# Moving half of two input groups into the next phase, merging two dimensions of the block scaling, and shifting a residual, a load and two coefficient chains in a convolution-scan kernel

## The chip, the cores and the metric

The kernel runs on one core of one Trainium2 chip. The metric is the device time of one execution in microseconds (us); the time of a kernel is the median of its runs.

## The reference

The input x has shape 32 x 48 x 64 x 128 (images, channels, rows, columns), fp32. Two layers are applied, each `x = x + conv(gn(x))`, where `gn` normalizes each image over groups of three channels, and `conv` is a chain of four scans. In each scan a line of the image is replaced by itself plus a 5-tap convolution over all 48 channels of the line before it, plus a bias:

```python
def step(w, b):
    def f(carry, inp):
        nxt = inp + _conv1d(carry, w, b)
        return (nxt, nxt)
    return f
...
_, d_rest = jax.lax.scan(step(down_w, down_b), d0, xs[1:])      # 64 rows, downwards
_, u_rest = jax.lax.scan(step(down_w, down_b), u0, seq)         # 64 rows, upwards
_, r_rest = jax.lax.scan(step(right_w, right_b), r0, ws[1:])    # 128 columns, rightwards
_, l_rest = jax.lax.scan(step(left_w, left_b), l0, R[Ww - 2::-1])  # 128 columns, leftwards
...
x = x + _L0_conv_ref(_gn(x), ...)
x = x + _L1_conv_ref(_gn(x), ...)
```

Each line needs the line before it, so the scans are one long chain of steps; only different images are independent.

## The kernel before

The 32 images are cut into four groups of eight (groups 0 to 3; the input of group g is called "input g" here and `x{g}` in the code). Row scans take one group at a time, column scans a pair of groups. `PHASES` (L103) puts them one after the other: phase 0 rows of group 0, phase 1 rows of group 1, phase 2 columns of pair 0, phase 3 rows of group 2, phase 4 rows of group 3, phase 5 columns of pair 1, and phases 6 to 11 the same for layer 1 (10 and 11 are the two column phases). Phases 8 and 9 are `JOINED` (L117): the downward scan of one group runs step by step together with the upward scan of the group before it; these are the joint scans.

A step (`step`, L904) is nine matrix products per scan direction and tile on TensorE (PE, L917) and three additions on VectorE (DVE, L931) that write the new line in place; the next step's products read them. In the program's names `step_02d` is layer 0, group 2, downwards; `00r` is layer 0, pair 0, rightwards; a number behind it is the line, and upward and leftward scans count down.

Everything else is put beside the steps by an agenda: `at(t, fn, ...)` asks for a function at step unit t, where a unit is one step (phase 1 starts at unit 126, phase 2 at 252, phase 3 at 506, phase 4 at 632). The agenda fixes the order of the instructions of each engine, and each engine runs its own in that order. Almost all DMAs are issued by SyncE (SP) from one queue; an issue whose data are not ready, or whose buffer is still in use, holds back all behind it.

What the change touches:

- `plan_input` (L1047) brings the raw input of groups 1 to 3 into the kernel's own layout, in six pieces of 2 MB. For each piece `take_in` (L658) loads it (DMA in_x to the buffer `nat`), `permute` (L675) reorders it in 16 copies on GpSimd (POOL), `put_out` (L677) stores it in four DMAs to the DRAM tensor `xin`, and `stats.take_others` takes sums on ScalarE (ACT, L544 to L536). Groups 2 and 3 have one buffer `nat`, so the next piece is loaded when the one before is used up. After the last piece `scaling` (L390) turns the sums into the scale and offset of the normalization: a chain of small operations over DVE (L561, L576, L465, L483, L495), PE (L401, L412), POOL and ACT. `spread` issues one of its operations per unit; its argument `slack` chooses between a short form on DVE (0) and a longer one that also uses POOL (8).
- `plan_rows` (L1067): `move_rows` (L713) loads 16 rows at a time from `xin` (20 DMAs; `ahead` says how many units before the scan, for each of the four blocks) and `scale_rows` (L753) normalizes them in place on ACT (24 activations at L760). In the joint scans blocks of eight rows are scaled. The result of a row phase is stored eight rows at a time by ten DMAs each (`upa` in layer 0); phase 0's stores are spread over phase 1, from unit 44 of it on.
- The seam between a row phase and a column phase (`send_row`, `send_rest`, L796, and `hold_queue`, L821): the first columns of pair 0 are gathered from the rows just finished by 91 small DMAs from on-chip memory to on-chip memory (`arena<-arena`). Half of them are issued by SP, behind all its stores. The first step rightwards waits for them.
- `plan_cols` (L1125): when a column phase is over, the result gets its residual in 24 units: `load_residual`, `add_residual` on POOL (L852), `keep_result` (a 1 MB store to `mid`), and sums for the next layer's normalization (on DVE for the first group of the pair, on ACT at L613 to L619 for the second). The last six of them (j = 0) come after the phase has ended, beside the next row phase. Then follow the two coefficient chains `r0` and `r1` (r2 and r3 for pair 1) for layer 1.

Of the kernel before, what the change touches and what calls it, by code (L numbers as in the profile page):

```python
# [41 lines left out]
GB = 8  # L42
# [35 lines left out]
def weight_runs():  # L78
# [24 lines left out]
PHASES = (  # L103
    ("rows", 0, 0),
    ("rows", 0, 1),
    ("cols", 0, 0),
    ("rows", 0, 2),
    ("rows", 0, 3),
    ("cols", 0, 1),
    ("rows", 1, 0),  # L110
    ("rows", 1, 1),
# [9 lines left out]
def kernel(  # L121
# [528 lines left out]
    x_masks = [mask_x]  # L650
# [38 lines left out]
    def row_views(k):  # L689
        return [slot[i].rearrange("p (o h n) -> p o h n", o=NG, h=HALF) for i in slots(k)]  # L690

    def place(k, h):


        first = k
        while first in JOINED:
            first -= 1
        since = k - first
        turned = (since + 1) // 2 % 2 if h < HALF else since % 2
        c = h % HALF // E8  # L700
        return HALF // E8 - 1 - c if turned else c

    def rows_at(k, h0, h1):

        places = sorted(place(k, h) for h in range(h0, h1, E8))
        at = places[0] * E8 + h0 % E8
        assert h0 // HALF == (h1 - 1) // HALF and places[-1] - places[0] == len(places) - 1
        return row_views(k)[h0 // HALF][:, :, at : at + h1 - h0]

    def row(k, h):  # L710
        return rows_at(k, h, h + 1)[:, :, 0]
# [41 lines left out]
    def scale_rows(k, h0, h1, groups=range(NG)):  # L753
        _, layer, g = PHASES[k]
        scale, offset = coeffs[layer, g]
        view = rows_at(k, h0, h1).rearrange("p o h (k b) -> p o b h k", b=GB)
        for o in groups:
            for b in range(GB):
                args = view[:, o, b], scale[:, o, b : b + 1], offset[:, o, b : b + 1]
                nc.scalar.activation(  # L760
                    args[0], args[0], AF.Identity, bias=args[2], scale=args[1]
                )
# [271 lines left out]
    def at(t, fn, *args):  # L1034
        agenda.append((t, len(agenda), fn, args))

    def spread(t, gen, every):


        def go(t):  # L1040
            if next(gen, "end") != "end":
                at(t + every, go, t + every)
                agenda.sort(key=lambda a: a[:2])

        at(t, go, t)

    def plan_input(g, times, work, lag, nats, perms):  # L1047

        stats = InputStats(f"x{g}", 0)
        rows = nats[0].shape[-1] // W  # L1050
        ahead, pieces_of = len(nats), rows * W // BN
        per = rows * W * GB // perms[0].shape[-1]
        for j, t in enumerate(times):
            nat = nats[j % ahead]
            if j == 0 and g > 1:
                at(t - 7, take_in, g, 0, nat)
            for i in range(per):
                perm, r = perms[i % len(perms)], i * rows // per
                at(t + i * work / per, permute, nat, r, perm, [nc.gpsimd])
                at(t + i * work / per + 4, put_out, g, rows * j + r, perm)  # L1060
            at(t + lag, stats.take_others, pieces_of * j, nat)
            if j + ahead < len(times):
                free = t + 7
                at(free, take_in, g, rows * (j + ahead), nat)
        spread(t + work + lag + (0, 2, 40, 32)[g], scaling(f"x{g}", 0, g, stats, x_masks, (0, 0, 8, 8)[g]), 1)

    def plan_rows(k, t0, prev):  # L1067
        down, up = (2 if k in JOINED else 1), (2 if k + 1 in JOINED else 1)
        t_up = t0 + down * (H - 1)
        if k == 1:  # L1070
            ahead, scaled = (-34, -18, -3, 12), (-12, -2, 17, 33)
        elif prev == "cols":
            ahead, scaled = (-28, -12, 4, 20), (-13, 3, 19, 35)
        else:
            ahead, scaled = (-54, -43, 0, 11), (-22, -8, 16, 30)
        if k in JOINED:
            for i in range(H // E8):
                h, t = i * E8, t0 + 2 * i * E8
                for o in range(NG):
                    at(t - 34 + 2 * o, take_rows, k, h, h + E8, o)  # L1080
                at(t - 17, scale_rows, k, h, h + E8)
        elif k:
            for i in range(4):
                if PHASES[k][1]:
                    for o in range(NG):
                        t = t0 + ahead[i] - 2 + 3 * o
                        at(t, take_rows, k, i * LOAD, (i + 1) * LOAD, o)
                else:
                    at(t0 + ahead[i], move_rows, k, i * LOAD, (i + 1) * LOAD, False)
                at(t0 + scaled[i], scale_rows, k, i * LOAD, (i + 1) * LOAD)  # L1090

        cuts = list(range(0, H + 1, E8))
        following = PHASES[k + 1][0] == "cols"
        seam = following and follows(k + 1)
        if seam:
            cuts = cuts[2:]
            end = t_up + up * (H - 1)
            at(end - E8, move_rows, k, E8, 2 * E8, True, 0)
            for h in range(E8 - 1, -1, -1):
                at(end - h, send_row, k + 1, h, range(0, E8 // 2))  # L1100
            at(end, send_rest, k + 1, range(E8 // 2, E8))
            for q in range(1, NQ):
                at(end + 0.1 if q == 1 else end + 1.6, move_rows, k, 0, 2 * E8, True, q)
        for h0, h1 in zip(cuts, cuts[1:]):
            t = t_up + up * (H - 1 - h0)
            if k == 0:
                t += 16 if h0 >= HALF else 68
            elif up == 2:
                t += 1
            elif not following:  # L1110
                t = t_up + 29 + 5 * (H - h1) / E8 + (34 if h1 <= HALF else 0)
            at(t, move_rows, k, h0, h1, True)
        at(
            t_up,
            nc.gpsimd.tensor_copy,
            last.rearrange("p (o n) -> p o n", o=NG),
            row(k, H - 1),
        )

    def follows(k):  # L1120

        _, layer, pair = PHASES[k]
        return PHASES[k - 1] == ("rows", layer, 2 * pair + 1)

    def plan_cols(k, t0, prev):  # L1125
        _, layer, pair = PHASES[k]
# [23 lines left out]
        end = left + W - 1  # L1150
        for i in range(n):

            t = left + 64 + 2 * i if layer == 0 else left + 39.5 + 4.5 * i
            at(t, spill_unit, k, i, True)
        units = []
        for n_done, j in enumerate((3, 2, 1, 0)):
            first, every = left + 34 + 32 * n_done, 4.5
            if j == 0 and PHASES[k + 1 if not final else k][0] == "rows":
                first, every = end + 29, 6
            units += [(first + every * i, j, i) for i in range(n)]  # L1160
        stats = None
        if layer == 0:
            stats = ResultStatsV(f"r{2 * pair}"), ResultStatsA(f"r{2 * pair + 1}")
# [6 lines left out]
        for u, (t, j, i) in enumerate(direct):  # L1170
            nat = tiles[u % n]
            o, half = UNITS[i]
# [24 lines left out]
                if u >= 2 and u - 2 + n < len(direct):  # L1197
                    at(t + 4.6, load_residual, k, *direct[u - 2 + n][1:], tiles[(u - 2) % n])
        if layer == 0:
            t = units[-1][0] + 14  # L1200
            g = 2 * pair
            spread(t, scaling(f"r{g}", 1, g, stats[0], r_masks, 8), 1)
            spread(t + 20, scaling(f"r{g + 1}", 1, g + 1, stats[1], r_masks, 8), 1)
# [24 lines left out]
    starts, end = [], 0  # L1228
    for k, (kind, *_) in enumerate(PHASES):
        n = (H if kind == "rows" else W) - 1  # L1230
        starts.append(end - 2 * n if k in JOINED else end)
        end = starts[-1] + (2 if k in JOINED else 1) * n + (2 if k + 1 in JOINED else 1) * n
    for k, (kind, layer, _) in enumerate(PHASES):
        (plan_rows if kind == "rows" else plan_cols)(k, starts[k], PHASES[k - 1][0])

    def wide_nat(i0, n):
        return arena[:, i0 : i0 + GB * n * W].rearrange("p (b m) -> p b m", b=GB)

    tiles = [stage[:, i] for i in range(4)]
    nats1 = [wide_nat(2 * SLOT + i * UNIT * 2, 4) for i in range(4)]  # L1240
    plan_input(1, [starts[0] + 44 + 7.5 * j for j in range(6)], 5, 1, nats1, tiles[2:4])
    nats = [wide_nat(3 * SLOT, 4)]
    times = [starts[1] + 24 + 9.5 * j for j in range(6)]
    plan_input(2, times, 6, 6, nats, tiles[2:4])
    times = [starts[2] + 60 + 13.5 * j for j in range(6)]
    plan_input(3, times, 6, 6, nats, tiles[2:4])

    def more_weights(key, layer, way):
# [12 lines left out]
    def first_group():  # L1261
# [124 lines left out]
        def scale_shared(h0, h1):  # L1386
            scale_rows(0, h0, h1, range(1))
            for o in range(1, NG):
                scale_at_once(0, h0, h1, pool, o, o + 1)
# [124 lines left out]
```

## Time and profile before

| | |
|---|---|
| time, median of 3 runs | 4370.5 us (4369.97 to 4374.02) |
| the profiled execution | 4372.83 us |
| its span, first to last instruction | 4371.1 us |
| mean granted TensorE clock | 0.968 |
| PE busy | 4063.2 us, 93% of the span |
| DVE, ACT, POOL busy | 2071.2, 1303.0, 829.9 us (47%, 30%, 19%) |
| DMA | 680.83 MB, 156 GB/s |

The profile was taken on one execution. A row of a timeline gives the start of a stretch of like instructions, how long the stretch lasted, engine, line and operation, the number of instructions, and in brackets the idle time ahead of it with what ended it. A row of a window gives each engine's busy time in it, then the granted clock, the mean busy share of the 16 DMA engines and GB/s. For SP (`SPq`) a row is the time over which a run of DMAs was issued, not the transfer itself. PE is busy for 93% of the span, so a change shows either as idle time of PE that goes or comes, or not at all.

### The profile page before, as it was taken

What the parts mean: (1) busy time and instruction counts of PE and PEld (TensorE: products, weight loads), DVE (VectorE), ACT (ScalarE), POOL (GpSimd) and SP (SyncE); (2) the same over time, 40 slices, a digit from 0 to 9 for tenths busy, and PEclk for the clock granted to TensorE, in tenths of its full rate; (3) what the DMA queues carried; (4) which work ended last, traced back from release to release, by engine and by line L of the source; (5) the groups of instructions that cost most, each with busy time, mean ns of one, the idle gap of its engine ahead of it and who ended that gap; (6) DMA issues with size and microseconds to landing.
All of it is one profiled execution on the core that took longest, in us unless ns stands there. A gap on an engine that the chain in (4) does not pass through costs nothing. (4 is left out here: it accounts for less than half of the span.)

```text
span 4371.1 us, 86080 instructions
## 1 busy us (share of the span) xinstructions
PE 4063.2 (93%) x34456; PEld 3962.1 (91%) x34456; DVE 2071.2 (47%) x6119; ACT 1303.0 (30%) x2632; POOL 829.9 (19%) x775
## 2 busy tenths in 40 slices
PE   7999929999999999999999997777899999999994
PEld 5999929999999999999999986666799999999994
DVE  6454414447664444446655432222244444444444
ACT  5646310336855100005773423223200002210022
POOL 5722220233220000004220000000000005530253
PEclk9999969999999999999999998988999999999997
DMA  9887797859989455807988845534389416999799
GB/s 291 235 168 166 181 163 144 247 154 263 197 164 151 72 99 108 206 1 217 216 152 137 128 76 80 82 63 79 56 136 176 115 49 165 290 269 164 137 241 192
DMA packets 2213584, 680.83 MB, mean 156 GB/s; under 512 B 2013776, under 2 KB 2162496, under 8 KB 2188608
## 3 DMA queue, kind: packets, MB, share of 16 engines
q1 hardware_dynamic: 2069056, 582.37, 65.0%
q10 hardware_dynamic: 141568, 87.46, 8.3%
q0 software_dynamic: 2560, 5.51, 0.5%
q8 instruction: 271, 4.44, 0.4%
q14 instruction: 129, 1.06, 0.1%
HBM read 398.29 MB, written 295.14 MB: 159 GB/s over the span
## 5 line engine op out<-in xcount | busy, mean ns | idle before, releaser
L760 ACT ACTIVATE arena<-arena,offset,scale 128x256 f32<-128x256 f32 (+2 forms) x936 | 589.8, 723 | 620.2 <-DVE arena L931 187.2
L852 POOL TENSOR_TENSOR arena<-arena 128x2048 f32<-128x2048 f32 x80 | 362.8, 4550 | 1493.8 <-PE step_10l L917 474.1
L917 PE MATMUL step_00r<-arena,early 128*128 128x128 f32 x2286 | 252.3, 274 | 78.4 <-DMA arena<-arena 77.6
L917 PEld LDWEIGHTS step_00r<-arena,early 128*128 128x128 f32 x2286 | 251.2, 185 | 79.1 <-issue 77.9
L675 POOL COPY arena<-arena 128x256 f32<-128x256 f32 x340 | 201.2, 651 | 416.3 <-DMA arena<-in_x 237.1
L613 ACT ACTIVATE early<-arena 128x256 f32<-128x256 f32 x192 | 129.6, 675 | 440.2 <-POOL arena L852 433.9
L917 PE MATMUL step_01r<-arena,early 128*128 128x128 f32 x2286 | 250.7, 273 | 7.0 <-DMA arena<-arena 5.9
L917 PEld LDWEIGHTS step_01r<-arena,early 128*128 128x128 f32 x2286 | 250.0, 185 | 7.7 <-issue 6.0
L917 PE MATMUL step_00l<-arena,wleft 128*128 128x128 f32 x2286 | 249.2, 272 | 0.0
L917 PE MATMUL step_11r<-arena,early 128*128 128x128 f32 x2286 | 249.2, 272 | 0.0
L917 PEld LDWEIGHTS step_11r<-arena,early 128*128 128x128 f32 x2286 | 248.6, 184 | 0.5 <-DVE arena L931 0.3
L917 PEld LDWEIGHTS step_00l<-arena,wleft 128*128 128x128 f32 x2286 | 248.7, 184 | 0.0
L917 PE MATMUL step_11l<-arena,wleft 128*128 128x128 f32 x2286 | 248.5, 272 | 0.0
L917 PE MATMUL step_10l<-arena,wleft 128*128 128x128 f32 x2286 | 248.5, 272 | 0.0
L917 PE MATMUL step_01l<-arena,wleft 128*128 128x128 f32 x2286 | 248.4, 272 | 0.0
L917 PE MATMUL step_10r<-arena,early 128*128 128x128 f32 x2286 | 248.4, 272 | 0.0
L917 PEld LDWEIGHTS step_10l<-arena,wleft 128*128 128x128 f32 x2286 | 248.4, 184 | 0.0
L917 PEld LDWEIGHTS step_11l<-arena,wleft 128*128 128x128 f32 x2286 | 248.4, 184 | 0.0
L917 PEld LDWEIGHTS step_01l<-arena,wleft 128*128 128x128 f32 x2286 | 248.4, 184 | 0.0
L917 PEld LDWEIGHTS step_10r<-arena,early 128*128 128x128 f32 x2286 | 248.4, 184 | 0.0
L931 DVE SCALAR_TENSOR_TENSOR arena<-step_00r,bd,arena 128x128 f32<-128x128 f32 x381 | 122.1, 348 | 209.5 <-PE step_00r L917 126.3
L874 ACT COPY arena<-arena 128x256 f32<-128x256 f32 x172 | 99.6, 656 | 368.8 <-POOL arena L852 243.5
(568 smaller groups left out, 6865.3 us busy)
## 6 DMA issues: line engine op xcount, KB each, us to landing
xin<-arena SPq DMA_DIRECT2D x94, 512.0 KB, 4.1
arena<-in_x SPq DMA_DIRECT2D x18, 2048.0 KB, 9.8
arena<-xin SPq DMA_DIRECT2D x96, 384.0 KB, 9.7
upb<-arena SPq DMA_DIRECT2D x192, 192.0 KB, 3.9
arena<-upb SPq DMA_DIRECT2D x96, 384.0 KB, 11.4
arena<-xin SPq DMA_DIRECT2D x174, 192.0 KB, 4.3
mid<-arena SPq DMA_DIRECT2D x32, 1024.0 KB, 11.6
upa<-arena SPq DMA_DIRECT2D x168, 192.0 KB, 3.9
```

The source lines that it names most:

```text
L613: nc.scalar.activation(junk[:, 0:n], view[:, b], AF.Identity, accum_out=self.sum[:, i, j : j + 1])
L675: copy(dst[:, r, q], src[:, r0 + r, q])
L760: nc.scalar.activation(args[0], args[0], AF.Identity, bias=args[2], scale=args[1])
L852: eng.tensor_tensor(unit, unit, nat, ALU.add)
L874: copy(by_w(perm)[:, a], src[:, a])
L917: nc.tensor.matmul(part(whole(ps[o])[0:m], -s), weights[:, i, at : at + m], part(src(i), s), start=seen[o] == 1, stop=seen[o] == left[o],)
L931: nc.vector.scalar_tensor_tensor(to, sums, bd[:, o, layer, way : way + 1], term, ALU.add, ALU.add)
```

## The change

There are five edits.

1. `scale_rows`: rows and the elements of a row are named as one merged dimension, `(h k)` in place of `h k`.
2. `plan_input`: for groups 2 and 3 every piece's load is placed seven units ahead of its permutation (before: the first only, and the others seven units behind the permutation of the piece before). The coefficient chain starts 2 (group 2) and 5 (group 3) units after the last piece, in place of 40 and 32, and group 3's chain has slack 0 in place of 8.
3. The six pieces of input 2 were all in phase 1, 9.5 units apart; now three are in phase 1, 16 apart from unit 28, and three in phase 2, 13 apart from unit 60. The six of input 3 were all in phase 2; now three are in phase 2 from unit 106 and three in phase 3 from unit 42.
4. `plan_rows`: where a row phase of layer 0 follows a row phase (phase 4; phase 1 has its own numbers), the first two blocks of rows are loaded 46 and 32 units ahead in place of 54 and 43.
5. `plan_cols` of pair 0: the six last residual units start at unit 3 behind the phase's end, 7 apart (before: 29 and 6), and the chains r0 and r1 start 70 units behind the last residual unit in place of 14.

```diff
@@ scale_rows
-        view = rows_at(k, h0, h1).rearrange("p o h (k b) -> p o b h k", b=GB)
+        view = rows_at(k, h0, h1).rearrange("p o h (k b) -> p o b (h k)", b=GB)
@@ plan_input
-            if j == 0 and g > 1:
-                at(t - 7, take_in, g, 0, nat)
+            if g > 1:
+                at(t - 7, take_in, g, rows * j, nat)
...
-            if j + ahead < len(times):
-                free = t + 7
-                at(free, take_in, g, rows * (j + ahead), nat)
-        spread(t + work + lag + (0, 2, 40, 32)[g], scaling(f"x{g}", 0, g, stats, x_masks, (0, 0, 8, 8)[g]), 1)
+            if g == 1 and j + ahead < len(times):
+                at(t + 7, take_in, g, rows * (j + ahead), nat)
+        t += work + lag + (0, 2, 2, 5)[g]
+        spread(t, scaling(f"x{g}", 0, g, stats, x_masks, (0, 0, 8, 0)[g]), 1)
@@ plan_rows
             ahead, scaled = (-54, -43, 0, 11), (-22, -8, 16, 30)
+            if not PHASES[k][1]:
+                ahead = (-46, -32, 0, 11)
@@ plan_cols
-                first, every = end + 29, 6
+                first, every = (end + 29, 6) if pair else (first, 7)
...
-            t = units[-1][0] + 14
+            t = units[-1][0] + (14 if pair else 70)
@@ the times of the pieces
-    times = [starts[1] + 24 + 9.5 * j for j in range(6)]
+    times = [starts[1] + 28 + 16 * j for j in range(3)]
+    times += [starts[2] + 60 + 13 * j for j in range(3)]
     plan_input(2, times, 6, 6, nats, tiles[2:4])
-    times = [starts[2] + 60 + 13.5 * j for j in range(6)]
+    times = [starts[2] + 106 + 13 * j for j in range(3)]
+    times += [starts[3] + 42 + 13 * j for j in range(3)]
     plan_input(3, times, 6, 6, nats, tiles[2:4])
```

Three places where the change moves instructions follow, as the built programs have them. The names: `arena` is on-chip memory, `in_x` the input, `xin_81` the DRAM tensor of input 2 in the kernel's layout, `upa_87` and `upa_88` the stored rows of phases 0 and 1.

On SP's queue in the second half of phase 1, the difference (minus is before, plus is after, numbers in the @@ lines are places in the two programs):

```order
@@ -249,5 +246,5 @@
 L287 DMA upa_87<-arena 48x32x32 x2
 L287 DMA upa_87<-arena 32x32x32
-L287 DMA xin_81<-arena 128x4x256 x2
+L287 DMA xin_81<-arena 128x4x256 x4
 L287 DMA upa_87<-arena 48x32x32 x2
 L287 DMA upa_87<-arena 32x32x32
@@ -257,6 +254,4 @@
 L287 DMA upa_87<-arena 48x32x32 x2
 L287 DMA upa_87<-arena 32x32x32
-L287 DMA xin_81<-arena 128x4x256 x2
-L287 DMA arena<-in_x 128x8x512
 L287 DMA upa_88<-arena 48x32x32 x2
 L287 DMA upa_88<-arena 32x32x32
```

The stores of the last pieces and the load of the sixth piece stood between the stores of finished rows; they are gone from there, and the row stores follow one another.

On DVE in phase 2, the start of the chain x2, which stood at the end of phase 1 before (first the rows of before, among the last steps upwards; `sum_x_x` holds ACT's sums of input 2):

```order
824 L931 SCALAR_TENSOR_TENSOR arena<-step_01u_5428,bd,arena 128x128
825 L561 TENSOR_REDUCE mean_x_x_5442<-sum_x_x_124 128x8
826 L562 TENSOR_SCALAR mean_x_x_5442<-mean_x_x_5442 128x8
827 L563 COPY mv_x_x_123<-mean_x_x_5442 128x8
828 L931 SCALAR_TENSOR_TENSOR arena<-step_01u_5451,bd,early 128x128
```

The same on DVE after, among the steps rightwards:

```order
1130 L931 SCALAR_TENSOR_TENSOR arena<-step_00r_7143,bd,arena 128x16x8
1131 L561 TENSOR_REDUCE mean_x_x_7157<-sum_x_x_124 128x8
1132 L562 TENSOR_SCALAR mean_x_x_7157<-mean_x_x_7157 128x8
1133 L563 COPY mv_x_x_123<-mean_x_x_7157 128x8
1134 L931 SCALAR_TENSOR_TENSOR arena<-step_00r_7161,bd,arena 128x16x8
```

After the change these three stand 306 rows further on, right behind the three additions of step 101 rightwards, and ahead of step 102's.

On ACT around the start of phase 3 (`offset`/`scale` of group 2; `sum_r`, `neg_r` and `dev_r` are the sums of r1), before and then after:

```order
-L760 ACTIVATE arena<-arena,offset_5780,scale_5779 128x256 x24
-L613 ACTIVATE early,sum_r_112<-arena 128x256 x8
-L616 ACTIVATE neg_r_113<-sum_r_112 128x8
-L619 ACTIVATE early,dev_r_114<-arena,neg_r_113 128x256 x8
-L760 ACTIVATE arena<-arena,offset_5780,scale_5779 128x256 x72
```

And on ACT after, from the same place:

```order
+L760 ACTIVATE arena<-arena,offset_7387,scale_7386 128x256 x24
+L613 ACTIVATE early,sum_r_112<-arena 128x256 x8
+L616 ACTIVATE neg_r_113<-sum_r_112 128x8
+L619 ACTIVATE early,dev_r_114<-arena,neg_r_113 128x256 x8
+L760 ACTIVATE arena<-arena,offset_7387,scale_7386 128x256 x24
```

Before, the second, third and fourth block of rows were scaled one behind the other (x72). After, sums of r1 stand between the first and the second block, and likewise between the second and the third and between the third and the fourth.

## The prediction

> **What bounds the kernel now.** I read the page's busy shares first, then the chain of waits by engine, PE's timeline where its idle time is long, and SP's timeline ahead of that place. PE carries the steps and is busy almost throughout, so its few gaps are what a change of order can win:
>
> ```profile
> PE 4063.2 (93%) x34456; PEld 3962.1 (91%) x34456; DVE 2071.2 (47%) x6119; ACT 1303.0 (30%) x2632; POOL 829.9 (19%) x775
> ```
>
> PE's timeline around the end of phase 1, and around the end of phase 4, the same seam for pair 1 (start, length; idle time ahead in brackets):
>
> ```profile
> 489.80 85.31 PE L917 MATMUL step_01u<-arena,early 128*128 128x128 f32 x776
> 652.73 14.47 PE L917 MATMUL step_00r<-arena,early 128*128 128x128 f32 x108 [77.62 <-DMA arena<-arena]
> ...
> 1539.76 122.95 PE L917 MATMUL step_03u<-arena,early 128*112 128x128 f32 x1119
> 1668.38 13.59 PE L917 MATMUL step_01r<-arena,early 128*128 128x128 f32 x108 [5.67 <-DMA arena<-arena]
> ```
>
> Phase 1 ends at 575.1 (489.80 + 85.31), and the first rightward step starts 77.62 us later, when the gathered columns have landed. The same seam costs 5.67 us in phase 5. So some 72 us of the first stall belong to what is queued ahead of the sends, not to the seam. SP's timeline in phase 1 shows the queue (start, time over which the run was issued, count):
>
> ```profile
> 330.60 42.44 SPq L287 DMA_DIRECT2D arena<-xin  x40
> 373.09 0.70 SPq L287 DMA_DIRECT2D arena<-in_x  x1
> 373.83 10.19 SPq L287 DMA_DIRECT2D wleft<-in_mask  x10
> 385.30 7.41 SPq L287 DMA_DIRECT2D xin<-arena  x4
> 395.83 0.37 SPq L287 DMA_DIRECT2D arena<-in_x  x1
> ...
> 427.10 15.65 SPq L287 DMA_DIRECT2D upa<-arena  x10
> ...
> 457.52 12.48 SPq L287 DMA_DIRECT2D early<-taps  x25
> 470.10 10.00 SPq L287 DMA_DIRECT2D upa<-arena  x10
> 480.14 3.30 SPq L287 DMA_DIRECT2D taps<-in_w  x5
> 483.95 13.16 SPq L287 DMA_DIRECT2D wleft<-taps  x25
> ...
> 502.09 18.22 SPq L287 DMA_DIRECT2D upa<-arena  x10
> ...
> 568.31 4.85 SPq L287 DMA_DIRECT2D arena<-upa  x7
> 573.26 18.86 SPq L287 DMA_DIRECT2D upa<-arena  x10
> 592.22 1.46 SPq L287 DMA_DIRECT2D arena<-upa  x3
> 593.78 42.47 SPq L287 DMA_DIRECT2D upa<-arena  x40
> 636.36 31.83 SPq L287 DMA_DIRECT2D arena<-arena  x47
> ```
>
> When the phase ends SP still has 50 row stores and ten loads to issue; the sends leave at 636.36 and PE restarts 16.4 us behind that. The DMA engines are full there (windows; the last three columns are clock, DMA share, GB/s):
>
> ```profile
> 500.00:550.00 50.00, 50.00 (x458) 50.00 (x457) 24.36 (x76) 16.97 (x46) 14.54 (x25) 1.00 0.98 235
> 550.00:600.00 50.00, 25.11 (x229) 24.92 (x227) 12.94 (x42) 8.07 (x21) 4.87 (x9) 0.79 1.01 190
> ```
>
> **The change part by part.** *Three pieces of input 2 out of phase 1.* This is the term that matters. A piece's DMA work is read from phase 2, where one piece runs alone in a period of 21 us:
>
> ```profile
> 855.00:876.00 21.00, 21.00 (x196) 21.00 (x195) 10.35 (x33) 12.53 (x34) 9.48 (x17) 1.00 0.58 201
> ```
>
> 0.58 x 21 = 12.2 us of all 16 engines, 36.5 us for three. SP gains in two ways: those transfers go, and SP no longer waits in order for a piece's permutation ahead of a row store. I walk the order after, with before's durations. The masks now stand ahead of the first load: 373.1 + 10.2 = 383.3. The first piece's cycle was 22.7 us (373.09 to 395.83), so the second piece loads at 406. Ten row stores at 10 to 15.65 us end at 416 to 422; taps, `early` and two stores of the piece end about 443; ten row stores 453; the third load, taps and `wleft` (3.3 + 13.2) 470; ten row stores 480; four stores of the last piece 484; ten row stores 494. Then stand 20 row stores, 7 loads, 10 stores, 3 loads, 40 stores. At 1.0 us a store (470.10: 10.00 for ten; 593.78: 42.47 for forty) that is 70 + 6.3, to 571; at the 1.8 us of the row at 573.26 for the first thirty it is 24 us more, 595. The last rows are finished only near 575, and the engines are full at least in part, so I choose the middle of 575 and 597, 586. PE restarts 16.4 us later, at 602, and idles 27 us instead of 77.6: **-50 us**. The ends are the 5.67 us of the seam at 1668.38 (-72) and sends as late as 597 with PE back at 613 or, with one more contended group of ten (18 us), 631 (-39 and -21).
>
> [...]
>
> *Input 2's other half in phase 2, input 3's in phases 2 and 3.* Phase 2 keeps six pieces at nearly the same units. Chain x2 now starts on DVE right behind step 101 rightwards, and DVE runs in order: if ACT's sums are late, that step's successors wait. In before the third piece of phase 2 stands at the same unit:
>
> ```profile
> L931 DVE SCALAR_TENSOR_TENSOR arena<-step_00r,bd,arena 128x128 f32<-128x128 f32 x303 | 97.1, 348 | 183.7 <-PE step_00r L917 100.5 <-DMA arena<-arena 83.2
> 859.03 0.22 ACT L552 ACTIVATE neg_x_x<-sum_x_x 128x8 f32<-128x8 f32 x1
> L483 DVE TENSOR_SCALAR var_x<-ps_x 128x24 f32<-128x24 f32 x1 | 0.2, 173 | 0.0
> ```
>
> The first row is for 640 to 857.2: 303 additions are 101 steps. The sums are done at 859.03: a wait of **+2 us**, 0 to 10 if the piece slips by half a period of 21. Chain x3 goes to phase 3 and mostly onto DVE, a dozen instructions more of some 0.2 us (the last row): +2.4 at most, and its work in phase 2 goes, so 0. Phase 3's own cost follows.
>
> *Residual units 26 units earlier (j = 0).* They hide in POOL and SP, but there they now stand ahead of phase 3's own rows. PE, SP, ACT of before around it, and the DMA share:
>
> ```profile
> 1158.09 124.65 PE L917 MATMUL step_02d<-arena,early 128*128 128x128 f32 x1134
> 1162.00 67.27 SPq L287 DMA_DIRECT2D arena<-xin  x57
> 1151.91 0.67 ACT L613 ACTIVATE early<-arena 128x256 f32<-128x256 f32 x1
> 1165.46 35.78 ACT L760 ACTIVATE arena<-arena,offset,scale 128x256 f32<-128x256 f32 x48
> 1219.46 17.96 ACT L760 ACTIVATE arena<-arena,offset,scale 128x256 f32<-128x256 f32 x24 [18.22 <-DMA arena<-xin]
> 1175.00:1200.00 25.00, 25.00 (x230) 25.00 (x230) 12.30 (x39) 25.00 (x35) 3.15 (x1) 1.00 0.98 177
> ```
>
> A step takes 124.65 / 63 = 1.98 us, so rows 32 are used from 1158.1 + 31.5 x 1.98 = 1220 and rows 48 from 1252. Before, they were scaled by 1201.2 and 1237.4: 19 and 15 us to spare. After, 14 more residual loads stand ahead of the third block and 10 loads with two 1 MB stores more ahead of the fourth. At 67.27 / 57 = 1.18 us each that is 16 and about 15 us, and ACT has a run of r1's sums (1151.91 to 1165.46, 13.6 us) between the blocks. ACT: second block to about 1186, sums to 1200, third block 1203 to 1221, sums to 1235, fourth 1238 to 1256. The third is late by 1, the fourth by 4: **+4 us**, from 0 (the loads drain faster) to 15 (the whole shift with no room).
>
> *Three pieces more in phase 3.* 36.5 us of DMA more, where before the windows from 1175 on show no room; what is pushed back is stores and phase 4's later rows, whose cover is SP's idle time in phase 4, 94 us before its last stores:
>
> ```profile
> 1451.20 6.74 SPq L287 DMA_DIRECT2D arena<-upa  x10
> 1551.68 99.69 SPq L287 DMA_DIRECT2D upa<-arena  x70
> ```
>
> So 0; without that cover it is rival (c). *Phase 4's first blocks 8 and 11 units later:* same cover. *Chains r0 and r1 56 units later:* they run beside steps both times and are needed in phase 6; their price is the longer upward scan of phase 3 against phase 4's:
>
> ```profile
> 1282.60:1413.70 131.10, 131.10 (x1197) 131.10 (x1196) 66.46 (x231) 49.05 (x68) 3.88 (x13) 1.00 0.97 147
> 1538.00:1662.70 124.70, 124.70 (x1137) 124.52 (x1135) 60.56 (x190) 0.00 (x0) 15.49 (x31) 1.00 0.60 103
> ```
>
> 6.4 us, paid wherever they stand: 0.
>
> *The merged dimension.* In the joint scans ACT does hold PE:
>
> ```profile
> L760 ACT ACTIVATE arena<-arena,offset,scale 128x128 f32<-128x128 f32 x376 | 192.6, 604 | 462.7 <-DVE arena L931 187.2 <-DMA upb<-arena 56.9 <-DMA arena<-mid 38.1
> 2540.00:3140.00 600.00, 471.88 (x2109) 395.35 (x2108) 162.45 (x356) 174.93 (x343) 1.01 (x2) 0.89 0.46 74
> ```
>
> PE is idle 128 of 600 us. But elements at stride 8, eight rows behind one another, are one dimension of 128 already in the program of before, and the built instructions are the same in address pattern, order and waits: 0.
>
> **Sum:** 4372.8 - 50 + 2 + 4 = 4328.8 against the profiled execution's own time, 4372.83 (span 4371.1, 1.7 outside it), which stands 2.3 us above the median of 4370.5; so 4326.5, given as **4327 us**.
>
> **The rivals.**
> (a) *The seam falls to that of phase 5.* Row stores at 1.0 us end at 571, and then only the 5.67 us stay. For it: the row at 470.10. Against: shares near 1. 4370.5 - 72 + 6 = 4305.
> (b) *The DMA engines set the sends.* The stores run at the contended rate and only part of the gain stays: -21 to -39 at the seam, +6: 4338 to 4356.
> (c) *Slower: phase 3 overflows.* Pieces, residual and rows share a queue with a DMA share of 0.97 already. The pieces of input 3 come late, DVE waits in order for their sums in chain x3 among the upward steps, and phase 4's scaling waits for the coefficients. Three pieces have 36.5 us of transfers in a full stretch; if each also costs its permutation in order (21 us a period, 63 us in all) and none is hidden, the loss exceeds the 44 us net gain by 19: 4390. It decides from 44 us of new stall on. Against it: the last residual unit is out of the way at unit 38, 1233; the sixth piece's load then leaves at about 1290 (two periods of 21 us or somewhat more), lands in 10 us and is summed in 13 (like r1's sums above) by 1313, while DVE asks for the sums behind the 23rd step upwards, 1282.6 + 23 x 1.98 = 1328: 15 us to spare.
> (d) *The merged view does something.* If it took the joint scans' wait for ACT, up to 128 us would go: 4199. The identical instructions speak against it.
>
> **How the numbers follow.** The forecast (seam stall of 20 to 38 us) has 0.60, (a) 0.15, (b) 0.13, (c) 0.10 of which half stays below no change by less than its price, (d) 0.02. About 0.2% (9 us) is what a measurement of this kernel can tell from no change. (c) gives 0.06 to slower, 0.03 to same and 0.01 to faster, and (b) 0.02 to same: faster 0.89, same 0.05, slower 0.06. The range reaches from (a) with 2 us less of cost, 4303, to the late end of (b), 4356.
>
> **What would show it.** In the profile after: PE's idle time ahead of the first `step_00r` at 20 to 38 us, SP's first `arena<-arena` at 577 to 597, three in_x loads in phase 1; a wait of a few us on DVE behind step 101 rightwards; PE idle for a few us in `step_02d` at rows 32 and 48, ended by ACT L760; the joint scans unchanged to the us. Wrong would be: the sends not before 610, a wait of over 20 us at L561 of chain x3, phase 4 starting on a wait for ACT L760, or PE's idle time in the joint scans smaller by more than a few us.

## The result and the profile after

The kernel after takes 4335.64 us (median of 6 runs, 4330.54 to 4340.08) against 4372.85 us for the kernel before, run beside it on the same chip (6 runs, 4369.97 to 4378.08). The ratio is 0.9914, with an interval of 0.9901 to 0.9927: 37.2 us less. The prediction was 43.5 us less, 4327, in a range of 4303 to 4356. A second set of four runs of the kernel after gave 4335.51 us and 0.9913 (0.9897 to 0.993). The profiled execution took 4338.45 us, its span is 4336.8.

The busy shares of the profile's page, after. Nearly the same work is done in a shorter span:

```profile
PE 4070.3 (94%) x34456; PEld 3969.8 (92%) x34456; DVE 2076.0 (48%) x6131; ACT 1303.4 (30%) x2632; POOL 826.5 (19%) x763
```

PE's timeline after at the seam of phase 1, in phase 3 and at the start of phase 5 (start, length; in brackets the idle time ahead and what ended it):

```profile
479.79 96.94 PE L917 MATMUL step_01u<-arena,early 128*128 128x128 f32 x882
603.79 17.05 PE L917 MATMUL step_00r<-arena,early 128*128 128x128 f32 x126 [27.06 <-DMA arena<-arena]
...
1108.16 95.25 PE L917 MATMUL step_02d<-arena,early 128*128 128x128 f32 x866
1208.02 32.61 PE L917 MATMUL step_02d<-arena,early 128*128 128x128 f32 x268 [4.62 <-issue]
...
1627.72 15.12 PE L917 MATMUL step_01r<-arena,early 128*128 128x128 f32 x108 [4.97 <-DMA arena<-arena]
1643.26 2.25 PE L917 MATMUL step_01r<-arena,early 128*128 128x128 f32 x18 [0.42 <-DVE arena L931]
1649.12 237.45 PE L917 MATMUL step_01r<-arena,early 128*128 128x128 f32 x2160 [3.60 <-DVE arena L931]
```

The stall of 77.62 us is now 27.06. Two gaps are larger: 4.62 us inside `step_02d`, which was 0, and 3.60 us in `step_01r`. The latter stood in before as well, smaller (PE's timeline, before):

```profile
1685.55 234.90 PE L917 MATMUL step_01r<-arena,early 128*128 128x128 f32 x2160 [1.08 <-DVE arena L931]
```

SP's timeline after shows why the seam is shorter:

```profile
402.60 15.25 SPq L287 DMA_DIRECT2D upa<-arena  x10
...
438.70 12.28 SPq L287 DMA_DIRECT2D upa<-arena  x10
...
472.18 9.38 SPq L287 DMA_DIRECT2D upa<-arena  x10
...
485.56 33.39 SPq L287 DMA_DIRECT2D upa<-arena  x30
519.05 3.43 SPq L287 DMA_DIRECT2D arena<-upa  x7
522.58 17.74 SPq L287 DMA_DIRECT2D upa<-arena  x10
540.42 1.55 SPq L287 DMA_DIRECT2D arena<-upa  x3
542.07 45.25 SPq L287 DMA_DIRECT2D upa<-arena  x40
587.42 31.76 SPq L287 DMA_DIRECT2D arena<-arena  x47
```

The sends leave at 587.42, not at 636.36, and PE restarts 16.4 us behind them, as before. The row stores that stood between pieces now follow one another, and the last forty begin 52 us sooner.

The windows after (each engine's busy time, then granted clock, DMA share, GB/s):

```profile
500.00:550.00 50.00, 50.00 (x458) 50.00 (x457) 24.06 (x76) 0.00 (x0) 0.00 (x0) 1.00 1.04 168
550.00:600.00 50.00, 26.73 (x244) 26.54 (x242) 13.42 (x42) 0.00 (x0) 15.18 (x30) 0.79 0.82 151
...
1200.00:1225.00 25.00, 20.39 (x158) 20.22 (x158) 8.70 (x27) 24.30 (x55) 10.49 (x17) 0.86 0.71 231
```

From 500 to 550 ACT and POOL have no work left, and the DMA engines are still full with finished rows alone (the stores, and the ten loads `arena<-upa`). In phase 3 the window with the gap has a granted clock of 0.86; in before all four windows from 1150 to 1250 have 1.00.

From PE's first start in each phase to its first start in the next, the two profiles differ as follows (us):

| where | before | after | difference |
|---|---|---|---|
| end of phase 1 | 575.1 | 576.7 | +1.6 |
| seam, PE idle | 77.6 | 27.1 | -50.6 |
| `00r` and `00l` | 505.4 | 504.4 | -1.0 |
| `02d` | 124.5 | 132.3 | +7.8 |
| `02u`, `03d`, `03u`, second seam | 385.8 | 387.3 | +1.4 |
| `01r` | 251.9 | 258.7 | +6.8 |

The first row is scatter: in the second profile of the kernel after phase 1 ends at 573.7. The rest of the kernel, the joint scans among it, adds up to -0.5. The rows add up to -33.9, the spans differ by -34.3.

### The profile page after: what moved, and what is told of

Its sections match the earlier page's. It is cut to its first block, busy times and chain, and to the rows that moved or that the text cites. A ratio compares the mean times of both kernels' runs of the same rounds, so it can differ in the third digit from the quotient of the medians.

```text
span 4336.8 us, 86029 instructions
## 1 busy us (share of the span) xinstructions
PE 4070.3 (94%) x34456; PEld 3969.8 (92%) x34456; DVE 2076.0 (48%) x6131; ACT 1303.4 (30%) x2632; POOL 826.5 (19%) x763
## 5 line engine op out<-in xcount | busy, mean ns | idle before, releaser
L917 PE MATMUL step_00r<-arena,early 128*128 128x128 f32 x2286 | 253.3, 274 | 28.2 <-DMA arena<-arena 27.1
L917 PEld LDWEIGHTS step_00r<-arena,early 128*128 128x128 f32 x2286 | 251.9, 185 | 29.2 <-issue 27.4
```

The lines of the kernel that those rows point to most:

```text
L917: nc.tensor.matmul(part(whole(ps[o])[0:m], -s), weights[:, i, at : at + m], part(src(i), s), start=seen[o] == 1, stop=seen[o] == left[o],)
```

## The experiments

The theory was: the gain is the seam, because three pieces less in phase 1 free the DMA engines for the row stores that stand ahead of the sends; the loss in phase 3 is the lateness of rows 48 behind the residual units; the other edits are what makes room for the pieces that were moved (of these only the residual's place was tested). The rivals were: SP's order is simply too long (the number of issues, not the transfers); the merged dimension does something; the residual's new place is not needed, or costs more than it gives; fewer pieces still in phase 1 are better.

**The merged dimension alone** (view_only). The kernel before with that one line of the change:

```diff
-        view = rows_at(k, h0, h1).rearrange("p o h (k b) -> p o b h k", b=GB)
+        view = rows_at(k, h0, h1).rearrange("p o h (k b) -> p o b (h k)", b=GB)
```

> The kernel before with the merged dimension in scale_rows as its only edit. My theory: nothing, 4373 us within 0.2%, the 600 us of the joint scans with PE busy 472 us as before, and the seam stall at 77 us. Rival: the merged view shortens ACT's wait in the joint scans, PE busy there rises above 480 us and the time falls by more than 9 us.

Measured: 4373.65 us (10 runs), ratio 0.9997 (0.9988 to 1.0007), the seam at 77.6 us, PE busy for 472.2 us of the 600 us of the joint scans (471.9 in before). The edit does nothing that shows, and the whole change lies in the order.

**Two pieces in phase 1** (two_pieces). Four of input 2 then stand in phase 2, and those of input 3 behind them:

```diff
-    times = [starts[1] + 28 + 16 * j for j in range(3)]
-    times += [starts[2] + 60 + 13 * j for j in range(3)]
+    times = [starts[1] + 28 + 16 * j for j in range(2)]
+    times += [starts[2] + 55 + 12 * j for j in range(4)]
...
-    times = [starts[2] + 106 + 13 * j for j in range(3)]
+    times = [starts[2] + 105 + 12 * j for j in range(3)]
```

> The kernel after with two pieces of input 2 in phase 1 instead of three, four in phase 2 (units 55, 67, 79, 91) and three of input 3 behind them. Theory (the sends wait behind what SP has in its queue, each piece taken out brings them forward by a third of 50.6 us, 17 us): PE idle ahead of the first rightward step falls from 27 to 10 us, time 4336 - 17 = 4319. Rival one (only the 12.2 us of DMA work of a piece count): 15 us idle, 4324. Rival two (the last row stores bound the sends, no piece matters any more): 27 us idle, 4336, or more if phase 2, with seven pieces, makes DVE wait for the sums of x2.

Measured: 4352.92 us, ratio 0.9948 (0.9933 to 0.9964), some 17 us slower than the kernel after. PE's timeline of this kernel:

```profile
592.37 13.92 PE L917 MATMUL step_00r<-arena,early 128*128 128x128 f32 x108 [19.28 <-DMA arena<-arena]
...
826.02 22.53 PE L917 MATMUL step_00r<-arena,early 128*128 128x128 f32 x180 [20.27 <-DVE arena L931]
```

and DVE's, where the second gap begins:

```profile
825.10 0.20 DVE L561 TENSOR_REDUCE mean_x_x<-sum_x_x 128x8 f32<-128x48 f32 x1 [20.92 <-ACT early L544]
```

The seam falls by another 8 us, and phase 2 pays 20: L561 stands in DVE's order among the steps and waits for ACT's sums of the last piece, which is late now that seven pieces share phase 2.

**Four pieces in phase 1**, two in phase 2 (four_pieces):

```diff
-    times = [starts[1] + 28 + 16 * j for j in range(3)]
-    times += [starts[2] + 60 + 13 * j for j in range(3)]
+    times = [starts[1] + 28 + 13 * j for j in range(4)]
+    times += [starts[2] + 73 + 13 * j for j in range(2)]
```

> The kernel after with four pieces of input 2 in phase 1 (13 units apart) and two in phase 2. Theory: idle ahead of the first rightward step 27 + 17 = 44 us, time 4353. Rival one (DMA work alone): 39 us, 4348. Rival two (the stores bound the sends): 27 us, 4336.

Measured: 4350.16 us, ratio 0.9946 (0.9931 to 0.9961). PE's timeline:

```profile
618.85 14.21 PE L917 MATMUL step_00r<-arena,early 128*128 128x128 f32 x108 [43.90 <-DMA arena<-arena]
```

With four, three and two pieces in phase 1, and the rest of the kernel after, the seam takes 43.9, 27.1 to 31.4 (six profiles of kernels with three) and 16.0 to 20 us. So the third piece taken out is worth 12 to 17 us, and the one after it some 10 (7 to 15, as the profiles scatter). With all six, in the kernel before, the seam takes 77.6: the first two are worth 34 us together, 17 each, but that step holds the other edits and the wider spacing too. The third is worth the 12.2 us of DMA work that the prediction gave a piece, or more, and the one after it on the average less.

**The residual units back at their old place**, the rest as after (resid_late). Pieces and residual rows use the same buffers, and in this kernel a piece overwrites a loaded residual:

```diff
-                first, every = (end + 29, 6) if pair else (first, 7)
+                first, every = (end + 29, 6)
```

> The kernel after with the last six residual units where they were before (29 units behind the phase, 6 apart); chains r0 and r1 follow them 70 units later. Theory (the early residual is what makes the third and fourth block of phase 3's rows late): the 4.6 us of PE idle time at row 48 goes and the downward scan of phase 3 takes 124.5 us instead of 132.2; the three pieces of input 3 then share their buffers with the residual, come some 10 to 20 us later, and DVE waits for their sums in chain x3 by 0 to 15 us in the upward scan: 4328 to 4343 in all. Rival one: the early residual costs nothing and the 7.8 us are scatter: downward scan 132, 4336. Rival two (the residual had to move, since the pieces come far too late without it): chain x3 or phase 4's scaling stalls PE by over 30 us, above 4358.

Measured: 4367.22 us, ratio 0.9983 (0.9974 to 0.9992). PE's timeline in phase 3:

```profile
1208.97 33.59 PE L917 MATMUL step_02d<-arena,early 128*128 128x128 f32 x288 [7.68 <-DVE arena L931]
1242.39 47.56 PE L917 MATMUL step_02u<-arena,early 128*128 128x128 f32 x432
1317.35 6.42 PE L917 MATMUL step_02u<-arena,early 128*128 128x128 f32 x36 [27.39 <-DVE arena L931]
```

and DVE's:

```profile
1313.52 0.20 DVE L561 TENSOR_REDUCE mean_x_x<-sum_x_x 128x8 f32<-128x48 f32 x1 [25.15 <-ACT early L544]
```

The gap in `step_02d` is another one than in the kernel after. ACT's and DVE's timelines show both sides of it:

```profile
1173.18 17.96 ACT L760 ACTIVATE arena<-arena,offset,scale 128x256 f32<-128x256 f32 x24 [21.17 <-DMA arena<-xin]
1208.05 0.62 DVE L589 BATCH_NORM_STATS2 bn_r<-arena 128x6 f32<-128x256 f32 x1 [8.34 <-POOL arena L852]
```

The fourth block of rows is scaled by 1191.14, some 16 us sooner than in the kernel after, and the wait for rows 48 is gone. So it was the residual's early place that made these rows late, as the theory said. In its stead DVE waits 8.34 us for the residual's addition on POOL, because the sums of the result (L589) stand in its order among the steps. And the last piece of input 3 comes too late for the chain x3: DVE waits 25.15 us, and PE 27.39. That is rival (c) of the prediction, kept away in the kernel after by the residual's new place.

**The weights on another queue** (weights_act). Sixty small DMAs of phase 1 (`taps`, `early`, `wleft`) are issued by ACT, which in the kernel after stands idle for 35.26 us there (from 424.15 to 459.41), and not by SP:

```diff
-        load_weights(key, layer, way)
+        load_weights(key, layer, way, on_act if (layer, key) in ((0, "right"), (0, "left")) else dma)
```

> The kernel after with the 60 small DMAs of the weights rightwards and leftwards (taps, early, wleft) issued by ACT's queue instead of SP's in phase 1. They move few bytes but hold SP for 39 us of its order (419.3 to 437.6 and 451.7 to 472.2). Theory (what delays the sends is the length of SP's order): the sends leave up to 20 us earlier, PE idle ahead of the first rightward step falls from 27 us to between 6 and 15, 4315 to 4324. Rival (the DMA engines' work sets it, and these DMAs have next to none): idle time stays at 27 us, 4336. Rival two (the last rows' stores are now the bound, as with two pieces): 19 us, 4328.

Measured: 4335.54 us, ratio 0.992 (0.9903 to 0.9936), like the kernel after. SP's timeline:

```profile
399.86 35.91 SPq L287 DMA_DIRECT2D upa<-arena  x10
...
486.32 33.50 SPq L287 DMA_DIRECT2D upa<-arena  x30
...
544.07 43.44 SPq L287 DMA_DIRECT2D upa<-arena  x40
587.61 32.05 SPq L287 DMA_DIRECT2D arena<-arena  x47
```

The queue is sixty issues shorter, and the sends leave at 587.61 in place of 587.42: the row stores take longer to issue instead (35.91 us for the first ten in place of 15.25). The seam takes 31.3 us, against 27.1 to 30.6 in the two profiles of the kernel after, and from 500 to 550 the DMA engines have a share of 1.02 (after: 1.04). SP's issues are not the bound here; the transfers behind them are.

**Phase 3's rows sooner** (rows_first). The second, third and fourth block of phase 3 are loaded 2, 4 and 8 units sooner than in the kernel after (units -12, 4 and 20 there):

```diff
+            if not PHASES[k][1]:
+                ahead = (-28, -14, 0, 12)
```

In this kernel (and in the one below that takes the edit over) the load of the third block overwrites rows of which the last residual sums are still to be taken, so the last of one unit's eight sums is taken of the wrong rows.

> The kernel after with the second, third and fourth block of phase 3's rows loaded 2, 4 and 8 units earlier, so that they stand ahead of four and three residual loads and one 1 MB store on SP's queue. Theory (the fourth block is late behind the residual): PE's 4.6 us at row 48 go, the granted clock no longer falls there, and the downward scan of phase 3 takes 124.5 us instead of 132.2: 4328. Rival (ACT's sums of r1 between the blocks are what delays the scaling): the wait stays at 3 to 5 us, 4336.

Measured: 4369.61 us, ratio 0.9994 (0.9984 to 1.0004). DVE's timeline:

```profile
1150.96 0.62 DVE L589 BATCH_NORM_STATS2 bn_r<-arena 128x6 f32<-128x256 f32 x1 [41.73 <-DMA arena<-xin]
```

PE loses 41.06 us in the third step of phase 3. The residual's sums (L589) stand in DVE's order and read the memory that the block is loaded into, so they wait for the load, and the step's additions wait behind them.

**Only the fourth block sooner**, at 5.5 in place of 20 (rows4):

```diff
+            if not PHASES[k][1]:
+                ahead = (-28, -12, 4, 5.5)
```

> The kernel after with only the fourth block of phase 3's rows loaded earlier, 5.5 units behind the phase's start instead of 20, so that it stands ahead of the last six residual loads and two 1 MB stores on SP's queue. Theory (the fourth block is late behind the residual's transfers): it lands some 12 us earlier, PE's 4.6 us at row 48 and the slow clock behind it go, the downward scan of phase 3 takes 124.5 to 126 us instead of 132.2, and the whole is 6 to 8 us faster than the kernel after. Rival (ACT's run of sums between the blocks sets it): the wait stays at 3 to 5 us. Rival two (the residual's sums on DVE, which wait in order, now come late): a DVE wait of over 8 us in that scan.

Measured: 4344.92 us, ratio 0.9932 (0.9917 to 0.9947), 9 us slower than after. PE's timeline, and DVE's at the same place:

```profile
1192.46 54.41 PE L917 MATMUL step_02d<-arena,early 128*128 128x128 f32 x468 [13.90 <-DVE arena L931]
```

```profile
1191.54 0.62 DVE L589 BATCH_NORM_STATS2 bn_r<-arena 128x6 f32<-128x256 f32 x1 [14.57 <-POOL arena L852]
```

Rows 48 are in time now and their gap is gone. In its place the residual, pushed back by the 20 loads, comes late for its own sums on DVE, and these hold the steps for 13.9 us. With the 7.68 us of resid_late, the gap of 4.62 us is the smallest of three prices for one queue.

**Two pieces, with more room for chain x2.** Both stand on top of the edit of two pieces. The first (two_late) starts the chain 14 units later, the first hunk below; the second (two_dve) also gives it the short form that leaves POOL out, the second hunk:

```diff
-        t += work + lag + (0, 2, 2, 5)[g]
+        t += work + lag + (0, 2, 16, 5)[g]
...
-        spread(t, scaling(f"x{g}", 0, g, stats, x_masks, (0, 0, 8, 0)[g]), 1)
+        spread(t, scaling(f"x{g}", 0, g, stats, x_masks, (0, 0, 0, 0)[g]), 1)
```

> The kernel with two pieces of input 2 in phase 1 again, and chain x2 14 units later, behind step 120 rightwards. Theory (DVE's 20 us wait at L561 was the only thing that phase 2's seventh piece cost): that wait is gone, the seam stays at 19 us, and the time is 4336 - 8 = 4328. Rival (seven pieces overload phase 2 in another place: the residual or phase 3's rows come late): a wait of over 8 us elsewhere, 4336 or more.

> The kernel after with two pieces of input 2 in phase 1 and four in phase 2, chain x2 14 units later and with slack 0, so that its small operations run on DVE instead of POOL, where they stood behind the next piece's permutation. Theory (POOL's order was what DVE waited for): no wait of DVE over 3 us in phase 2, seam at 16 to 20 us, 8 to 11 us faster than the kernel after. Rival (phase 2 cannot hold seven pieces): again a wait of some 20 us, and 4340 or more.

Measured: 4344.04 us, ratio 0.9934 (0.9919 to 0.9949), and 4370.64 us, ratio 0.9994 (0.9985 to 1.0004). The seams are 16.0 and 19.3 us. DVE's timeline of the first, then of the second:

```profile
868.70 0.20 DVE L576 TENSOR_REDUCE var_x_x<-neg_x_x 128x8 f32<-128x48 f32 x1 [20.39 <-POOL neg_x_x L572]
```

```profile
894.10 0.30 DVE L447 RECIPROCAL std_x<-std_x 128x24 f32<-128x24 f32 x1 [45.03 <-ACT std_x L444]
```

The wait for the sums is gone and comes back one engine further on. In the first kernel an operation of the chain on POOL stands behind the permutation of the next piece, which waits 8.44 us for its load and then takes 9.26 us. In the second POOL is out of the chain, and the one operation left on ACT (L444) stands behind the sums of the next pieces, for whose loads POOL's copies wait 8.59 and 12.09 us; that ACT waits for the same loads is argued from its order.

**Combinations.** Two_late with the blocks of rows_first and the weights on ACT (all_three); two_dve with the fourth block of rows4 (best):

> The three edits of weights_act, rows_first and two_late together. If the seam goes down to the 5 us of phase 5 and the 7.8 us of phase 3 go too: 4336 - 22 - 8 = 4306. If the seam is bound by the last rows' stores at about 19 us: 4336 - 8 - 8 = 4320. If weights on ACT's queue hold up ACT's scaling or sums: above 4336.

> The edits of rows4 and two_dve together: if both theories hold, 14 to 19 us faster than the kernel after, about 4319.

Measured: 4375.57 us (ratio 1.001) and 4382.43 us (ratio 1.0016, 1.0006 to 1.0025). Both add up what their parts cost: PE gaps of 44.2 us in `step_02d` and 16.2 in `step_00l`, and of 44.4 in `step_00l` and 17.1 (two gaps) in `step_02d`. No kernel tried is faster than the one after by more than the runs scatter.

**The kernel after once more**, for the scatter of its gaps (after_again):

> The kernel after once more, for the rows that scatter. In its first profile the rightward scan of phase 5 took 258.6 us, in the kernel before 251.8, though the order and the waits are the same. If that belongs to the change, it is 258 to 259 again; if it is scatter, 252 to 253 can come, and the total is then nearer 4331 than 4339.

Measured: 4335.51 us; seam 30.6 us, gap in `step_02d` 3.3 us, `01r` 258.0 us.

## Why the prediction was right, and where its sum was off

*The seam* (-50 forecast): -50.6. The sends were put at 586 and left at 587.42; PE idles 27.06 us for the 27 given. The mechanism was right, but that it was met so closely is in part luck. The walk through SP's order gave 571 to 595, the range used 597 for the late end, and 586 was chosen as the middle of 575 and 597, not worked out; in the second profile of the kernel after the sends leave at 588.11 and PE idles 30.57 us. The dose of pieces shows the cause: from four to three and from three to two, with the same other edits, the stall falls each time. What is only argued is why the three pieces gave 17 us each and not 12.2: a piece also spreads the row stores, but no run takes its transfers and its place in the order apart.

*Rival (a), the seam of phase 5*: with two pieces the sends leave at 573.26 at the earliest (two_late), and PE restarts 16.1 us behind them. Phase 5 reaches 4.97 us because its sends leave some 11 us before the phase ends (SP 1612.09, PE's last step 1622.75). Freeing the DMA engines alone does not give that. *Rival (b)*: the contended rate of 1.8 us a store held for ten stores only (17.74 us), not for the thirty that this rival needs; thirty others went out in 33.39 us and the last forty in 45.25, 1.1 us each.

One reading of the lines was off, and it does not enter the sum: at the end of phase 1 in before three loads stand in SP's queue and not ten, since the run of seven was issued from 568.31 to 573.16.

*Chain x2* (+2 forecast): 0. ACT's timeline has the last of the sums at 803.29, and DVE's asks for them at 805.92:

```profile
803.29 0.19 ACT L544 ACTIVATION_READ_ACCUMULATOR early<-arena 128x1 f32 x1
```

```profile
805.92 0.19 DVE L561 TENSOR_REDUCE mean_x_x<-sum_x_x 128x8 f32<-128x48 f32 x1
```

They are in time by 2.4 us, no more: two_pieces shows the stall that stands behind that margin.

*Rows 48 in phase 3* (+4 forecast): the place, the row block and the mechanism were right, and the size of the term was not. ACT's timeline has the scaling of the third and the fourth block, and DVE's the wait for it:

```profile
1152.30 18.00 ACT L760 ACTIVATE arena<-arena,offset,scale 128x256 f32<-128x256 f32 x24 [5.03 <-DMA arena<-xin]
1189.65 17.88 ACT L760 ACTIVATE arena<-arena,offset,scale 128x256 f32<-128x256 f32 x24 [5.77 <-DMA arena<-xin]
1207.57 0.35 DVE L931 SCALAR_TENSOR_TENSOR arena<-step_02d,bd,arena 128x128 f32<-128x128 f32 x1 [4.83 <-ACT arena L760]
```

The fourth block's scaling ends at 1207.53 and PE goes on at 1208.02, after 4.62 us. ACT had been idle for 5.77 us until the block's load was there, so the load behind the residual set the time, and not ACT's run of sums. At rows 32, where 1 us was forecast, PE shows no gap. But `02d` is longer by 7.8 us: the window from 1200 has a clock of 0.86 where the prediction reckoned with full speed on both sides of the gap. That is 3.2 us beyond the gap, so a change shows not only as idle time of PE but also in the clock behind it.

*Rival (c), chain x3*: its sums were done at 1279.4 and asked for at 1286.4, 7 us to spare where the prediction reckoned 15. Resid_late, with the residual at the old place, shows it happen, at 27 us. The condition named, that the last residual unit is out of the way, was the one that decides.

*The chains r0, r1 and x3* (0): `02u` -1.2, `03d` +3.3, and `00l`, where chain x3 stood before, -2.4: what leaves one phase comes in another, -0.3 in sum. *The merged dimension* (0, rival (d)): 0, by view_only.

*Not foreseen*: 6.8 us in `01r`. DVE waits 4.99 us for the last sent columns, ahead of the additions of step 7, where in before it waits 2.47 (DVE's timeline, before and then after):

```profile
1685.14 0.87 DVE L931 SCALAR_TENSOR_TENSOR arena<-step_01r,bd,arena 128x128 f32<-128x128 f32 x3 [2.47 <-DMA arena<-arena]
```

```profile
1648.71 0.87 DVE L931 SCALAR_TENSOR_TENSOR arena<-step_01r,bd,arena 128x128 f32<-128x128 f32 x3 [4.99 <-DMA arena<-arena]
```

The order of the instructions there is the same in both programs. `01r`, from its first start to its last, takes 251.8 to 252.9 us in seven profiles (before, view_only, weights_act, rows_first, two_late, all_three, best), where PE's gap ahead of step 8 is 0.8 to 1.1 us, and 257.9 to 258.7 in the seven others (the kernel after both times), where that gap is 3.6 to 4.6. Between before and after the gap is 2.5 of the 6.8 us, and the rest goes with a lower clock behind it: in after 0.82 and 0.91 in the two windows of 25 us from 1625, in before 0.93 and 1.00 in those from 1666. The change does not force the long value, since five of the twelve profiles that contain it have the short one. Whether it makes it more likely, and why the last columns come later, stays open.

What was off is therefore the sum and not the mechanism: forecast -50 + 2 + 4 = -44; found between the two profiles -50.6 + 0 + 7.8, +6.8 in `01r`, and +2.1 in the small rest, -33.9. The medians differ by -37.2; the profiled execution after lies 2.8 us above its median.

Not tried: the input pieces moved without the residual and the chains, the chains r0 and r1 back behind the last residual unit, phase 4's first blocks back at their old units, chain x3 in its long form, and three pieces at the old spacing. The value of edit 4 and of the chains' new place is therefore argued, not shown.

## What to carry to other kernels

When a phase ends in a long stall behind a full DMA queue, take transfers out of that phase one by one and watch the stall: here the third was worth 12 to 17 us, and the gain of the fourth was lost again where it arrived. In the phase that receives them, look first at the engine that carries the step chain: any operation that stands in its order and waits for a transfer, directly or over another engine, stops the chain for the whole wait (8 to 45 us in the runs here). Price a gap in a chain of matmuls with the clock behind it too: here gaps of 3.3 to 4.8 us cost 1.9 to 3.3 us more than themselves, while around one of 1.08 us the clock stayed at 1.00.

## What was not expected of the hardware

In six profiles (after, after_again, two_pieces, four_pieces, two_late, weights_act) a gap of 3.3 to 4.8 us in `step_02d` lengthened that phase by 5.2 to 7.8 us, 1.9 to 3.3 us beyond the gap itself. In the kernel after PE stands from 1203.40 to 1208.02; the granted clock is 1.00 up to 1207, 0.60 in the two us to 1209, 0.50 to 1213, 0.70 to 1215 and 1.00 again behind that. A window of 25 us around the gap has 0.86 in it, and 0.93 in weights_act; that is an estimated 25 x 0.14 = 3.5 and 25 x 0.07 = 1.8 us of lost clock, and the two phases lost 3.2 and 1.9. The longest matmul of the phase took 550 to 555 ns in four of the six and 435 and 436 in two (weights_act and after_again), against 335 in before; the four lost 2.8 to 3.3 us, the two 1.9.

In `01r` a gap of 1.08 us goes with 251.8 us and one of 3.60 us with 258.6. Around the first (before, 1680 to 1690) every window of 2 us has a clock of 1.00; behind the second (after) it is 0.50 from 1649 to 1653, 0.62 in the two us to 1655 and 1.00 again behind that. The shortest of these gaps with a loss is the one of 3.26 us (after_again), with 1.9 us behind it. From what length on a gap costs clock was not shown.

From 500 to 550 stores and loads of finished rows alone keep the DMA engines of the kernel after at a share of 1.04 with 168 GB/s; taking three pieces away lowered the bytes (235 GB/s in before) and not the share (0.98 in before).
